# The first expert block and the last batch's attention steps of a two-layer kernel, in another order

## The chip, the cores and the metric

The kernel runs on one core of a Trainium2 chip. The core has a matrix engine (PE, whose weight loads are shown apart as PEld), three engines for elementwise work (DVE, ACT, POOL) and a queue for transfers (SP). POOL issues the scattered transfers too. Each engine runs its own instructions in their order and waits on semaphores for the others. The metric is the device time of one execution in microseconds (us), the median of several runs.

## The reference

The input is 8 batches of 512 tokens with 128 features. Two layers follow each other, each with a residual sum, `x = x + attention(xn) + ffn(xn)`. The first layer has a causal attention with 16 heads and a soft mixture of 8 experts. The second layer, in which the change lies, has a differential attention and a mixture of 8 experts that takes the two best experts for each token:

```python
# differential attention, per batch
diff = softmax(q1 @ k1.T * scale) - lam_full * softmax(q2 @ k2.T * scale)
out  = diff @ v
out / sqrt(mean(out * out) + EPS) * (1 - LAMBDA_INIT)
...
# experts: the rows sent to one expert stand together, at most 1280 of them
act     = gelu(einsum('ech,ehf->ecf', exp_in, moe_w1))     # 128 -> 512
exp_out = einsum('ecf,efh->ech', act, moe_w2)              # 512 -> 128
moe     = zeros.at[padded_ids].add(exp_out * padded_probs[:, None])
```

## The kernel before

Up to 874 us of the span the kernel does the first layer, the second layer's small attention and routing (which writes each token's row with its two weights and its number into the buffer `xs` in DRAM, line 910), and the differential attention of batches 0 to 6 (`diff`, line 1354). The differential attention of the eighth batch, number 7, is held back (`LATE`). It is a generator, `late`, and each `next` on it issues one step. There are 21: two products with the folded weights (`diff_qk`), one for the values (`diff_v`), eight scores (`diff_scores`: a product on PE of 512 columns, a maximum on DVE, an Exp on ACT), four with transposes (`diff_T`), one in which nothing is issued, four with the product with the values (`diff_out`, the last with four small operations on POOL, lines 1333 to 1336 and 129), and the end (`diff_end`, four rows on DVE, line 1342). `diff_both`, the difference of the two softmaxes on DVE, goes with a neighbouring step.

The rest of the kernel is the experts. Each of the 8 experts has 1280 slots, ten chunks of 128 rows, in three blocks of 4, 4 and 2 chunks; `BLOCKS` lists all 24. For each expert `rows_get` (line 1422) loads its rows into the tile `xe` on SP's queue, two experts ahead, and `rows_in` (line 1429) computes on DVE the weight and the token number of each row. For each block there are three steps.

- `expert_T` (line 1443): PE transposes the chunks, and DVE copies them with the layer norm's weight and bias into `xeT` (line 1447).
- `expert_up` (line 1451), called twice for a block: two products with the first weights on PE (line 1458; each is two matmul instructions in the trace) and a Gelu on ACT into `hT` (line 1461). Exp and Gelu need different tables in ACT; a load of the table is an instruction of its own in the trace.
- `expert_down` (line 1463), called for each half of the chunks: four products for each chunk into one tile of PSUM (line 1473; 16 instructions for two chunks). With the last half DVE scales each chunk into `es` (line 1481), and POOL adds each chunk's rows to the output by an indirect transfer (line 1486), 80 of them in all.

The stores of an expert may add to rows that the expert before has added to. So each store waits until all ten of the expert before have landed (lines 1493 and 1494). Batch 7's attention is added to the output by one direct transfer on POOL (`late_add`, lines 1503 to 1516) after the last block of expert 6. It waits for expert 6's stores and expert 7's stores wait for it.

What order the instructions of PE, DVE, ACT and POOL have is written by hand: `in_order` (line 244) ties each instruction to the one before it on its engine, as the program issues them. SP's queue isn't tied so. The loop at lines 1528 to 1542 is a pipeline. In block m it issues the two ups of block m+1, the transposes of block m+2, and the two halves of the down of block m, and, from block 6 on, two late steps in the first half and one in the second:

```python
for hp in range(2):
    expert_up(*BLOCKS[m + 1], hp)
    if hp == 1: expert_T(*BLOCKS[m + 2])      # rows_in first, for a new expert
    expert_down(e, c0, n, half[hp])
    late_steps(((2,1)[hp]) if m >= 6 else 0)
```

Ahead of the loop stand, in this order, the loads of experts 0 and 1, `rows_in(0)`, the transposes of blocks 0 and 1, and the two ups of block 0.

Of the kernel before, what the change touches and what calls it, by code (L numbers as in the profile page):

```python
# [18 lines left out]
P = 128  # L19
# [6 lines left out]
def kernel(ctx: ExitStack, tc: tile.TileContext, a: dict, out: bass.AP):  # L26
    nc = tc.nc
# [10 lines left out]
    CAP = 1280  # L38
    NCT = CAP // P
# [10 lines left out]
    def psum_s(name):  # L50
        return ps["s"].tile([P, 2, 512], F32, tag="s", name=name)

    def psum_o(name, pool="o"):
        return ps[pool].tile([P, 512], F32, tag="o", name=name)
# [9 lines left out]
    for b in range(NB):  # L64
# [9 lines left out]
        out=se, in_=a["L0_ffn_slot_embeds"].rearrange("e s d -> (e s) d").rearrange("(c p) d -> p c d", p=P)  # L74
# [10 lines left out]
    for n, key in enumerate(("L0_attn_qln_w", "L0_attn_qln_b", "L0_attn_kln_w", "L0_attn_kln_b")):  # L85
        nc.sync.dma_start(
            out=lnrow[n : n + 1], in_=a[key].unsqueeze(0).unsqueeze(0).to_broadcast([1, H, S])
# [10 lines left out]
    for e in range(NE):  # L98
        nc.sync.dma_start(
            out=b2c[(e % 2) * NS : (e % 2 + 1) * NS, e // 2, :],  # L100
            in_=a["L0_ffn_b2"][e : e + 1].to_broadcast([NS, D]),
# [10 lines left out]
    for n, v in enumerate((-0.5, -1.0)):  # L112
# [7 lines left out]
        out=cmask[:, 384:512], in_=cmask[:, 384:512], pattern=[[-1, P]],  # L120
# [17 lines left out]
    def transpose4(name, blocks, pool="t"):  # L138
        t = psum_t(name, pool)
        for k, blk in enumerate(blocks):  # L140
            nc.tensor.transpose(t[:, k * P : (k + 1) * P], blk, ident)  # L141
        return t

    xs = dram.tile([NE * CAP, W], F32, name="xs")
# [473 lines left out]
    sync = mybir.DependencyInfo(mybir.DependencyClass.Sync, mybir.DependencyReason.DATA)  # L618
    puts = []
# [622 lines left out]
    with ExitStack() as l1b:  # L1242
# [178 lines left out]

        def rows_get(e):
            xe = wk.tile([P, NCT, W], F32, tag="xe", name=f"xe_{e}", bufs=3)
            get = nc.sync.dma_start(out=xe, in_=xs[e * CAP : (e + 1) * CAP].rearrange("(c p) d -> p c d", p=P))
            for name in puts:
                tc.add_manual_dep(get.ins, name, sync, reason="any token may be in this expert's slots")
            ee["xe", e] = xe

        def rows_in(e):

            xe = ee["xe", e]
            first = small.tile([P, NCT], F32, tag="first", name=f"first_{e}", bufs=2)
            nc.vector.tensor_scalar(
                out=first, in0=xe[:, :, D + 3], scalar1=float((NE - e) * CAP), scalar2=None, op0=ALU.is_equal
            )
            wt_ = small.tile([P, NCT], F32, tag="wt", name=f"wt_{e}", bufs=2)
            nc.vector.tensor_tensor(out=wt_, in0=first, in1=xe[:, :, D + 1], op=ALU.mult)
            nc.vector.tensor_tensor(out=wt_, in0=wt_, in1=xe[:, :, D], op=ALU.add)
            to = small.tile([P, NCT], U32, tag="to", name=f"to_{e}", bufs=4)
            nc.vector.tensor_scalar(out=to, in0=xe[:, :, D + 2], scalar1=FAR, scalar2=None, op0=ALU.add)  # L1440
            ee["wt", e], ee["to", e] = wt_, to

        def expert_T(e, c0, n):
            w = n * P
            t = transpose4(f"xeT_p{e}_{c0}", [ee["xe", e][:, c0 + k, :D] for k in range(n)])
            ee["xeT", e, c0] = xeT = wk.tile([P, T], F32, tag="xeT", name=f"xeT_{e}_{c0}")
            nc.vector.tensor_scalar(  # L1447
                out=xeT[:, :w], in0=t[:, :w], scalar1=cols[:, 2:3], scalar2=cols[:, 3:4], op0=ALU.mult, op1=ALU.add
            )

        def expert_up(e, c0, n, hp):
            w, xeT = n * P, ee["xeT", e, c0]
            if hp == 0:
                ee["hT", e, c0] = wk.tile([P, NHC, T], F32, tag="hTm", name=f"hTm_{e}_{c0}")
            ph = psum_s(f"phm_{e}_{c0}_{hp}")
            for k in range(2):
                hc = 2 * hp + k
                nc.tensor.matmul(  # L1458
                    ph[:, k, :w], lhsT=w1_1[:, e, hc * P : (hc + 1) * P], rhs=xeT[:, :w], start=True, stop=True
                )  # L1460
            nc.scalar.activation(ee["hT", e, c0][:, 2 * hp : 2 * hp + 2, :w], ph[:, :, :w], AF.Gelu)  # L1461

        def expert_down(e, c0, n, ks):
            hT = ee["hT", e, c0]
            if c0 == 0 and ks[0] == 0:
                ee["es", e] = wk.tile([P, NCT, D], F32, tag="es", name=f"es_{e}", bufs=4)
                backs.append([])
            if ks[0] == 0:
                ee["pe"] = psum_o(f"pem_{e}_{c0}")
            pe, es = ee["pe"], ee["es", e]  # L1470
            for k in ks:
                for hc in range(NHC):
                    nc.tensor.matmul(  # L1473
                        pe[:, k * D : (k + 1) * D], lhsT=hT[:, hc, k * P : (k + 1) * P], rhs=w2_1[:, e, hc, :],
                        start=(hc == 0), stop=(hc == NHC - 1),
                    )
            if ks[-1] < n - 1:
                return
            for k in range(n):
                c = c0 + k  # L1480
                nc.vector.tensor_scalar(
                    out=es[:, c], in0=pe[:, k * D : (k + 1) * D], scalar1=ee["wt", e][:, c : c + 1], scalar2=None,
                    op0=ALU.mult,
                )

                back = nc.gpsimd.indirect_dma_start(  # L1486
                    out=out_rows, out_offset=bass.IndirectOffsetOnAxis(ap=ee["to", e][:, c : c + 1], axis=0),
                    in_=es[:, c], in_offset=None, bounds_check=NB * T - 1, oob_is_err=False,
                    compute_op=ALU.add,
                )  # L1490
                tc.declare_no_dep(back.ins, group=f"backs{e}", reason="an expert's rows differ")
                tc.add_to_no_dep_group(f"backs{e}", back.ins)
                for name in backs[e] if e else bases:
                    tc.add_manual_dep(back.ins, name, sync, reason="a row is read and written by each addition")
                backs[e + 1].append(back.ins.name)
# [3 lines left out]
        def late_steps(n):  # L1499
            for _ in range(n):  # L1500
                next(late, None)

        def late_add(e):

            for _ in late:
                pass
            new = []
            for b in LATE:
                add = nc.gpsimd.dma_start(
                    out=out[b].rearrange("(i p) d -> p i d", p=P),  # L1510
                    in_=dd["po", b].rearrange("p (i d) -> p i d", i=NI), accum_op=ALU.add,
                )
                for name in backs[e + 1]:
                    tc.add_manual_dep(add.ins, name, sync, reason="a row is read and written by each addition")
                new.append(add.ins.name)
            backs[e + 1] = new

        BLOCKS = [(e, c0, min(4, NCT - c0)) for e in range(NE) for c0 in range(0, NCT, 4)]
        AFTER = 6
        rows_get(0)  # L1520
        rows_get(1)
        late_steps(0)
        rows_in(0)
        expert_T(*BLOCKS[0])
        expert_T(*BLOCKS[1])
        expert_up(*BLOCKS[0], 0)
        expert_up(*BLOCKS[0], 1)
        for m, (e, c0, n) in enumerate(BLOCKS):
            if c0 == 0 and e + 2 < NE:
                rows_get(e + 2)  # L1530
            half = range(n // 2), range(n // 2, n)
            for hp in range(2):
                if m + 1 < len(BLOCKS):
                    expert_up(*BLOCKS[m + 1], hp)
                if hp == 1 and m + 2 < len(BLOCKS):
                    if BLOCKS[m + 2][1] == 0:
                        rows_in(BLOCKS[m + 2][0])
                    expert_T(*BLOCKS[m + 2])
                expert_down(e, c0, n, half[hp])
                late_steps(((2,1)[hp]) if m >= 6 else 0)  # L1540
            if e == AFTER and c0 + n == NCT:
                late_add(e)
        in_order(tail)
# [37 lines left out]
```

## Time and profile before

| what | value |
|---|---|
| median of 3 runs | 1081.13 us (1080.82 to 1083.46) |
| the profiled execution | 1080.87 us |
| its span, first to last instruction | 1079.2 us |
| PE busy over the span | 964.9 us (89%) |
| DVE, ACT, POOL busy over the span | 677.6, 561.3, 569.0 us |
| PE and POOL busy from 897 to 1053 us | 153.9 and 111.9 of 156 us |
| PE and POOL busy from 1053 us to the end | 0.0 and 15.5 of 26.2 us |
| stores of the experts (line 1486) | 80, mean 1555 ns, from 897.7 to 1073.5 us |
| table loads in the experts' part | 7 for Gelu, 6 for Exp, 1283 ns each |

The span is what the profile covers; the execution's time is 1.67 us longer than its span. Times inside the span are counted from its start. A row of the timeline has the start and duration of an instruction or of a few merged ones, its engine, its line, the operation, what it writes and reads, and, in brackets, how long its engine sat idle before it and which instruction released it. An engine's idle time counts only where it delays what ends last. For that the chain of waits is followed back from the last instruction.

### The profile page before, as it was taken

The numbers are of one execution on the slowest core, as the hardware profiler recorded it, in microseconds if no ns is written. First come the engines' busy times: TensorE is split into PE (matmuls) and PEld (weight loads), VectorE is DVE, ScalarE is ACT, GpSimd is POOL, SyncE is SP. The second block draws the span as 40 slices with busy tenths as digits, with TensorE's granted clock in tenths as the row PEclk, the third lists the DMA queues.
The fourth block names the chain that finished last, engine by engine and source line by source line (L and its number), as shares of the span: only waits on it lengthen the run. The fifth ranks groups of instructions, "written<-read, shape, count | busy, mean of one in ns | idle before, by whom it ended". The sixth has DMA issues, their size and how long they took to land.

```text
span 1079.2 us, 18766 instructions
## 1 busy us (share of the span) xinstructions
PE 964.9 (89%) x6702; PEld 594.3 (55%) x6702; DVE 677.6 (63%) x2130; ACT 561.3 (52%) x1261; POOL 569.0 (53%) x794
## 2 busy tenths in 40 slices
PE   7889899989999999999899999878678879999990
PEld 3457556857545455545444445345445657777780
DVE  6634643377777788888878788359887642243230
ACT  3466347363366566767565655526346552393220
POOL 3201000200242537785878978876877635667775
PEclk9899999999699999999999999859889999999995
DMA  8630000000000000000000000050000143332213
GB/s 253 153 92 2 1 1 1 2 1 2 1 1 2 1 2 2 19 4 2 9 14 2 22 1 22 2 173 1 10 20 16 30 110 58 50 50 36 26 10 34
DMA packets 49838, 33.23 MB, mean 31 GB/s; under 512 B 12248, under 2 KB 44803, under 8 KB 49744
## 3 DMA queue, kind: packets, MB, share of 16 engines
q1 hardware_dynamic: 34832, 24.80, 8.6%
q0 software_dynamic: 14096, 6.97, 4.9%
q8 instruction: 53, 0.87, 0.3%
q14 instruction: 41, 0.34, 0.1%
q10 hardware_dynamic: 816, 0.26, 0.1%
HBM read 17.56 MB, written 17.33 MB: 32 GB/s over the span
## 4 chain that ended last, share of the span: by engine, by line
PE 62%; POOL 13%; DVE 13%; issue 5%; ACT 3%; DMA 2%; POOLq 0%; SPq 0%; DVEq 0%; ACTq 0%
PE se L1082 11%; PE phm L1458 6%; PE pem L1473 6%; PE po L1107 5%; PE sm L1049 4%; PE lg_d L316 3%; PE pe L491 3%; PE psl L360 3%; DVE junk L1059 3%; PE s L1287 3%; PE pf L393 2%; POOL xs L910 2%; PE pq L969 2%; PE lg_c L316 2%; PE ph L465 2%
## 5 line engine op out<-in xcount | busy, mean ns | idle before, releaser
L1059 DVE CUSTOM_DVE_ANT_0 junk<-sm,cmask 128x128 f32<-128x128 f32 (+3 forms) x512 | 249.7, 488 | 68.9 <-PE sm L1049 30.5
L1087 ACT ACTIVATE pt<-se 128x384 f32<-128x384 f32 (+1 forms) x384 | 185.7, 527 | 158.7 <-PE sm L1049 110.0
L1049 PE MATMUL sm<-kj,qT 32*128 32x256 f32 (+3 forms) x1024 | 231.5, 483 | 5.4 <-ACT kj L643 2.7
L1082 PE MATMUL se<-q,kj 32*128 32x128 f32 (+3 forms) x1024 | 210.2, 477 | 4.0 <-DVE mcol L1059 3.5
L1486 POOL DMA_INDIRECT out_dram<-es,to x80 | 124.4, 1555 | 61.9 <-issue 28.4
L1082 PEld LDWEIGHTS se<-q,kj 32*128 32x128 f32 x1024 | 99.8, 189 | 86.9 <-DVE mcol L1059 25.2
L1092 POOL TENSOR_SCALAR_AFFINE_SELECT pt<-pt 128x512 f32<-128x512 f32 (+1 forms) x96 | 80.0, 833 | 115.2 <-ACT pt L1087 115.0
L1049 PEld LDWEIGHTS sm<-kj,qT 32*128 32x128 f32 x1024 | 111.4, 190 | 24.4 <-DVE mcol L1059 10.3
L1107 PE MATMUL po<-pt,vpad 128*18 128x512 f32 (+3 forms) x1024 | 92.0, 455 | 12.0 <-POOL pt L1092 12.0
L1461 ACT ACTIVATE hTm<-phm 128x1024 f32<-128x1024 f32 (+1 forms) x48 | 42.4, 882 | 79.0 <-PE phm L1458 78.8
L1458 PE MATMUL phm<-xeT,w 128*128 128x512 f32 (+1 forms) x192 | 78.7, 534 | 4.1 <-DVE xeT L1447 3.6
L1473 PEld LDWEIGHTS pem<-w,hTm 128*128 128x128 f32 x640 | 77.0, 192 | 7.6 <-issue 7.2
L1291 ACT ACTIVATE ex<-s,nm 128x512 f32<-128x512 f32 x64 | 43.9, 687 | 69.2 <-DVE nm L1290 68.7
L1473 PE MATMUL pem<-w,hTm 128*128 128x128 f32 x640 | 78.9, 275 | 0.0
L910 POOL DMA_INDIRECT xs<-l_z,sput x64 | 67.3, 1051 | 17.9 <-issue 15.4
L1287 PE MATMUL s<-xn,qk 128*128 128x512 f32 x128 | 69.4, 662 | 7.1 <-ACT qk L1265 3.9
L522 POOL TENSOR_TENSOR x_all<-x_all,bo_bc 128x512 f32<-128x512 f32 x8 | 10.2, 1276 | 121.4 <-DVE xn L280 121.4
L1447 DVE TENSOR_SCALAR xeT<-xeT_p,cols 128x512 f32<-128x512 f32 (+1 forms) x24 | 17.2, 721 | 73.9 <-PE xeT_p L141 73.9
L1107 PEld LDWEIGHTS po<-pt,vpad 128*18 128x18 f32 x1024 | 20.7, 97 | 62.8 <-POOL pt L1092 23.7
L1290 DVE TENSOR_REDUCE nm<-s 128x1 f32<-128x512 f32 x64 | 43.0, 683 | 17.0 <-PE s L1287 16.7
L1458 PEld LDWEIGHTS phm<-xeT,w 128*128 128x128 f32 x192 | 34.0, 194 | 27.0 <-issue 21.6
L736 POOL TENSOR_TENSOR l_prod<-l_qkv 128x512 f32<-128x512 f32 x36 | 46.3, 1298 | 3.2 <-DVE l_at L630 1.9
(270 smaller groups left out, 1872.4 us busy)
## 6 DMA issues: line engine op xcount, KB each, us to landing
xs<-cmask SPq DMA_DIRECT2D x1, 5280.0 KB, 24.1
xe<-xs SPq DMA_DIRECT2D x8, 660.0 KB, 4.4
x_all<-in_L_attn_x_dram SPq DMA_DIRECT2D x8, 256.0 KB, 4.6
w<-in_L_ffn_w_dram SPq DMA_DIRECT2D x1, 2048.0 KB, 8.9
w<-in_L_ffn_moe_w_dram SPq DMA_DIRECT2D x1, 2048.0 KB, 9.8
out_dram<-x_all SPq DMA_DIRECT2D x8, 256.0 KB, 2.2
out_dram<-es,to POOLq DMA_INDIRECT x80, 3.2
xs<-l_z,sput POOLq DMA_INDIRECT x64, 2.3
```

Of the source, the lines that this page charges most:

```text
L316: nc.tensor.matmul(lg, lhsT=lhs(k), rhs=rhs, start=True, stop=True)
L910: put = nc.gpsimd.indirect_dma_start(out=xs, out_offset=bass.IndirectOffsetOnAxis(ap=sput[:, k, m : m + 1], axis=0), in_=z2[:, i], in_offs ...
L1049: nc.tensor.matmul(sc[:, o : o + w], lhsT=st["qT", b][rr, i * P : (i + 1) * P], rhs=st["k", b, j][rr, :w], start=True, stop=True,)
L1059: nc.vector.tensor_tensor_reduce(out=junk[:, :w], in0=sc[:, o : o + w], in1=cmask[:, 512 - w : 512], scale=-1.0, scalar=BIG, op0=ALU.add, ...
L1082: nc.tensor.matmul(sc[:, o : o + w], lhsT=st["k", b, j][rr, c * P : (c + 1) * P], rhs=st["q2", b, (g % G) // 2][rr, c * P : T], start=True ...
L1087: nc.scalar.activation(st["pt", g, k][:, r, :o], sc[:, :o], AF.Exp)
L1092: nc.gpsimd.affine_select(out=pt[:, :, :n, :P], in_=pt[:, :, :n, :P], pattern=[[0, 4], [0, n], [1, P]], compare_op=ALU.is_ge, fill=0.0, ba ...
L1107: nc.tensor.matmul(po[32 * r : 32 * r + 2 * PW, c * P : T], lhsT=vpads[b % 3][:, c, at_ : at_ + 2 * PW], rhs=pt[:, r, o : o + w], start=(c ...
L1287: nc.tensor.matmul(sc, lhsT=dd["qk", b, k][:, i * P : (i + 1) * P], rhs=xnT[:, b], start=True, stop=True)
L1458: nc.tensor.matmul(ph[:, k, :w], lhsT=w1_1[:, e, hc * P : (hc + 1) * P], rhs=xeT[:, :w], start=True, stop=True)
L1473: nc.tensor.matmul(pe[:, k * D : (k + 1) * D], lhsT=hT[:, hc, k * P : (k + 1) * P], rhs=w2_1[:, e, hc, :], start=(hc == 0), stop=(hc == NH ...
L1486: back = nc.gpsimd.indirect_dma_start(out=out_rows, out_offset=bass.IndirectOffsetOnAxis(ap=ee["to", e][:, c : c + 1], axis=0), in_=es[:, ...
```

## The change

It has three parts. The load of expert 0's rows is split into two transfers, of four and of six chunks. In front of the loop block 0's transposes go ahead of `rows_in(0)`, and block 1's transposes go behind block 0's ups; block 0's whole down, with its es and its four stores, then comes ahead of the ups of block 1 and the transposes of block 2. The late steps are issued one per block, in its first half, from block 3 on. By block 20 that is 18 steps; the remaining three (the last two products with the values, with the four small operations on POOL, and the end) are issued in `late_add`, which runs the generator to its end.

```diff
         def rows_get(e):
             xe = wk.tile([P, NCT, W], F32, tag="xe", name=f"xe_{e}", bufs=3)
-            get = nc.sync.dma_start(out=xe, in_=xs[e * CAP : (e + 1) * CAP].rearrange("(c p) d -> p c d", p=P))
-            for name in puts:
-                tc.add_manual_dep(get.ins, name, sync, reason="any token may be in this expert's slots")
+            rows = xs[e * CAP : (e + 1) * CAP].rearrange("(c p) d -> p c d", p=P)
+
+            for c0, c1 in ((0, 4), (4, NCT)) if e == 0 else ((0, NCT),):
+                get = nc.sync.dma_start(out=xe[:, c0:c1], in_=rows[:, c0:c1])
+                for name in puts:
+                    tc.add_manual_dep(get.ins, name, sync, reason="any token may be in this expert's slots")
...
         late_steps(0)
+        expert_T(*BLOCKS[0])
         rows_in(0)
-        expert_T(*BLOCKS[0])
-        expert_T(*BLOCKS[1])
         expert_up(*BLOCKS[0], 0)
         expert_up(*BLOCKS[0], 1)
+        expert_T(*BLOCKS[1])
         for m, (e, c0, n) in enumerate(BLOCKS):
...
             half = range(n // 2), range(n // 2, n)
+            if m == 0:
+
+                expert_down(e, c0, n, range(n))
             for hp in range(2):
...
-                expert_down(e, c0, n, half[hp])
-                late_steps(((2,1)[hp]) if m >= 6 else 0)
+                if m > 0:
+                    expert_down(e, c0, n, half[hp])
+                late_steps(((1,0)[hp]) if m >= 3 else 0)
```

## The prediction

> **What bounds the kernel now.** The change lies behind 874 us, so I read the end of the chain of waits first. From 884 us on it runs through PE at line 1473 and line 1458 block after block, and only from 1035 us through POOL's stores (line 1486). So I put the timelines of POOL, DVE and ACT beside each other. Columns: start, duration, engine, line, operation, and in brackets the idle time before it with its releaser.
>
> ```profile
> 897.68 1.68 POOL L1486 DMA_INDIRECT out_dram<-es,to  x1 [16.05 <-DVE es L1481]
> ...
> 914.53 1.55 POOL L1486 DMA_INDIRECT out_dram<-es,to  x1 [0.31 <-issue]
> 919.67 1.55 POOL L1486 DMA_INDIRECT out_dram<-es,to  x1 [3.58 <-issue]
> ...
> 957.63 1.61 POOL L1486 DMA_INDIRECT out_dram<-es,to  x1 [0.30 <-issue]
> 965.15 1.55 POOL L1486 DMA_INDIRECT out_dram<-es,to  x1 [5.92 <-DVE es L1481]
> ...
> 982.10 1.55 POOL L1486 DMA_INDIRECT out_dram<-es,to  x1 [0.30 <-issue]
> ...
> 989.53 1.64 POOL L1486 DMA_INDIRECT out_dram<-es,to  x1 [2.15 <-DVE es L1481]
> ...
> 1047.85 1.54 POOL L1486 DMA_INDIRECT out_dram<-es,to  x1 [0.30 <-issue]
> 1051.35 1.39 POOL L1509 DMA_DIRECT2D out_dram<-po  x1 [1.96 <-DMA out_dram<-es,to]
> 1056.76 1.64 POOL L1486 DMA_INDIRECT out_dram<-es,to  x1 [4.03 <-DMA out_dram<-po]
> ```
>
> The 80 stores on POOL are the spine from 897.68 to the end. Ten stores of an expert take 16.6 to 17.0 us from first to last start. Then the next expert waits until they have landed: from last start to next start 5.14 (into expert 1), 4.32 (2), 4.70 (5) and 3.68 us (6), mean 4.46. Two steps are longer, 7.52 us into expert 3 and 7.43 us into expert 4, and there DVE's es is the releaser: PE was late. For expert 3 the row on DVE is:
>
> ```profile
> 964.52 1.13 DVE L1481 TENSOR_SCALAR es<-pem,wt 128x128 f32<-128x128 f32 x4 [1.24 <-PE pem L1473]
> ```
>
> The first es of experts 0 to 7 start at 897.04, 916.01, 936.69, 964.52, 988.89, 1007.86, 1026.82 and 1045.79. Without late steps PE needs 18.96 us per expert (1007.86 to 1026.82), less than POOL's 21.1. With the late steps of batch 7 crowded into blocks 6 to 12 it took 27.83 and 24.37. So PE bounds experts 3 and 4, the landing of the stores all others.
>
> **The first block.** Before it, this row order on DVE decides:
>
> ```profile
> 881.67 1.13 DVE L1347 SCALAR_TENSOR_TENSOR x_all<-po,ri,x_all 128x128 f32<-128x128 f32 x4 [5.30 <-POOL ri L129]
> 882.71 0.17 DVE L1433 TENSOR_SCALAR first<-xe 128x10 f32<-128x10 f32 x1
> ...
> 883.29 1.52 DVE L1447 TENSOR_SCALAR xeT<-xeT_p,cols 128x512 f32<-128x512 f32 x2
> ```
>
> *Split load.* I cost it at nothing: PE transposes xe at 879.55, so it has landed by then, and DVE is shut until 882.7 by batch 6's last rows. One more SP issue (0.36 us) stands ahead of expert 1's load, which isn't read before some 901.8. If that cover went, the earlier landing would be worth at most what 396 of 660 KB take at some 300 GB/s, 1.3 us.
>
> *Transposes ahead of rows_in.* Four DVE operations (882.71 to 883.29) leave the front of xeT: 0.58 us earlier. PE starts line 1458 at 883.57 instead of 884.15; eight matmuls took 5.24 us (half of it at a granted clock of 0.5), so they end at 888.81, and the second gelu ends at 890.03 (890.61 before).
>
> *Block 0's down in one go.* Block 1's transposes (0.44) now stand here, then PE waits for that gelu, idle some 0.95 us, which block 1's up covered before. The 32 down matmuls take 3.73 us (the row at 1049.10): 890.2 to 893.93. es starts then, the first store 0.64 later as before: 894.6, 3.1 us earlier. But block 1 pays: two ups 3.44, T 0.22, then PE waits for xeT (1.1 us from the transposes' start) where a down covered it before, 0.86 idle; up 0.87, two half downs 3.58 with up and T (1.30) between, 0.17 to the last one's end. es of block 1 starts at 904.25, before 902.78: **1.47 later**. POOL, through its first four stores at 901.9, waits for it: fifth store 904.88 (905.26 before), tenth 914.15 (914.53). So of 3.1 us some 0.4 are left.
>
> **The late steps.** The generator has 21 steps. Before: three a block from block 6, done at 12. After: one a block from 3 to 20, and the last three (two out steps, the end) in late_add. PE prices from starts in the trace: a score or qk 0.86, v 0.89, four transposes 0.43, out 0.89. I set each expert's first es, by PE, against POOL (last start + 4.46), es + 0.64 giving the store:
>
> - expert 1: PE 916.01 + 1.47 + 0.86 (qk) = 918.34, store 918.98; POOL 918.61. Start 918.98.
> - expert 2: + 18.96 + 0.86 + 0.89 + 0.86 = 939.91, store 940.55; POOL 918.98 + 16.72 + 4.46 = 940.16. Start 940.55 (940.71 before).
> - expert 3: + 18.96 + three scores 2.58 + 0.9 stall (below) = 962.35, store 962.99; POOL 961.93. Start 962.99 (965.15).
> - expert 4: + 18.96 + 2.15 = 983.46, store 984.10; POOL 962.99 + 16.95 + 4.46 = 984.40. Start 984.40 (989.53).
> - expert 5: POOL 1005.58, PE 1004.78. Expert 6: POOL 1026.65, PE 1025.49. Start 1026.65 (1031.24).
>
> **The table loads.** Dealt singly, eight scores switch ACT between Exp and Gelu 16 times, before 12 times. What decides is whether a load waits for the exp's data:
>
> ```profile
> 941.86 1.28 ACT L1291 ACT_TABLE_LOAD   x1 [2.76 <-DVE nm L1290]
> ...
> 946.53 1.28 ACT L1291 ACT_TABLE_LOAD   x1
> 948.23 0.69 ACT L1291 ACTIVATE ex<-s,nm 128x512 f32<-128x512 f32 x1 [0.42 <-DVE nm L1290]
> ```
>
> Only the first did (it has a separate semaphore instruction, the last of that line at 941.8); the one at 946.53 ran ahead. With T0 the start of a score on PE: exp at T0 + 1.83, gelu 2.15 after it, 0.6 or 1.02 long: hT is ready at T0 + 4.63 to 5.05. PE, with up, T, half down and up between, asks for it at T0 + 5.46, 5.67 or 5.88, by the block's place in its expert: no stall. The first one, 1.28 later, stalls PE 0.9. If all loads waited, the stalls would be 0.9, 0.2 and 0.45 by place, 3.75 in all for blocks 6 to 11, 13 and 14. Bounds 0 and 3.75; I take 0.9, by the row at 946.53.
>
> **The addition of batch 7.** Its four ri operations now stand on POOL behind expert 6's tenth store, 1043.26. From the rows at 982.10 and after: store 1.55, ri ready 3.53 after the store's start, DVE's four rows 1.05, release 0.3: the addition starts 4.88 after that store, where landing alone needed 3.50. **Cost 1.38.** The outs on PE end near 1040, some 4 us before POOL asks. Addition at 1048.14 instead of 1051.35; what follows (5.41, ten stores, the end) is unchanged.
>
> **Sum.** 3.2 us off the profiled span of 1079.2: 1076.0. That execution took 1080.87 us, 1.67 around the span and 0.26 below the median of 1081.13. On the median: **1077.9 us**. Everything hangs on two near ties, PE against POOL, at 0.1 to 1.2 us.
>
> **Rivals.**
>
> *All Exp loads wait for data* (above): 2.85 more on PE, expert 6 at 1028.34, 2.9 earlier than before, less 1.38: **1079.6**. For it: 27 of 48 gelus and the first exp have a separate wait. Against it: the five later loads all began before their nm had ended. 0.2.
>
> *PE's clock doesn't drop in the first block.* It did after an idle time of 3.56 us (880.59 to 884.15), and came back within 888 to 889; the granted clock is the third number from the end of this stretch:
>
> ```profile
> 885.00:886.00 1.00, 1.00 (x2) 0.34 (x1) 0.00 (x0) 0.00 (x0) 0.00 (x0) 0.53 0.04 8
> ```
>
> Now PE is idle 0.07 us less (0.44 later transposes, 0.58 earlier start: 880.08 to 883.57, 3.49). A shorter idle time, 874.7 to 876.5, left the clock at 1.00. Without the drop the first four matmuls end at 885.4 (four at 0.43 and 0.15), the load (1.28) and two gelus (2.17) behind them at about 889.0, 1.0 earlier, and PE, which bounds experts 1 to 3, carries that through: **1076.9**. 0.2. The Trainium skill (TensorE: Matmul & The Clock Gate, "What's actually happening") says that a free-running window of about 3.4 us that is idle halves the clock, and a busy one restores it; the trace's drop, 885.0 to 888.4, is as long, and by that rule 3.49 us of idle time may or may not hold such a window.
>
> *A switch of tables costs more than its load.* This is the way to the slower side. Its place is each score step, between exp and gelu. With x us more per switch, the first of a pair is hidden up to 1.1, the second takes the spare 0.41, 1.04 and 0.83 by place. The nearest row for x is the load itself, 1.28. Both together then delay hT by 1.45: stalls of 1.04, 0.41 and 0.62, 5.2 in all, and 2.4 more at the unhidden first load; PE is then 6.7 beyond my sum at expert 6, which starts at 1032.2: **1083.4**, and over 1084.4 from x = 1.34 on. It is slower than before once PE is 4.4 beyond my sum there. Against it: the load at 946.53 starts 0.01 after the gelu before it, and the gelu behind the load of 949.09 at 950.38, 0.01 after the load's end. 0.08. The Trainium skill (ScalarE: Activation LUTs, "What ACT_TABLE_LOAD costs") gives 1283 ns for the load, as here, and some 1.38 us of draining besides, which by the working above would make some 1085; by its advice to batch by set, dealing scores out singly is the wrong direction. No row here shows the draining.
>
> **How the numbers follow.** Forecast 0.52, waiting loads 0.2, no drop 0.2, dearer switches 0.08. The forecast's own spread is about 1.2 us: a landing wait of 3.7 or 5.1 instead of 4.46 moves the boundaries behind expert 3 by up to 0.7 each, and PE's lead, 0.3 to 1.2 us, caps the gain. A change of 0.3% (3.24 us, to 1077.89) is about what a measurement of this kernel can tell from none, and the forecast lies on that line: half of it counts as faster, half as same. Faster 0.26 + 0.2 = 0.46; same 0.26 + 0.2 and a quarter of the dearer switches, 0.48; slower 0.06. The range runs from 1075.0 (no drop, no stall at the first load, and landings so short that PE alone bounds expert 6: 1.0, 0.9 and 1.2 less, rounded) to 1081.2 (all loads waiting, 1079.6, and landings of 5.1 behind expert 3); outside lie the dearer switches and some 5 in 100 on either side.
>
> **What would show it.** First store near 894.6 from the span's start (allowing for a shift of all that lies before 874), but a gap of about 3 us between the fourth and fifth; PE idle before the first line 1473 and before block 2's line 1458. Starts of experts 3, 4 and 6 earlier by about 2, 5 and 4.6. 16 table loads, Exp's ahead of their data but for one, and no PE wait on ACT beyond 1 us. Lines 1335 and 129 behind expert 6's tenth store, and about 4.9 us from that store to the addition. I am wrong if PE's 18.96 us per expert without late steps isn't kept, if waits on ACT appear at each score, or if the landing waits grow because expert loads (after each expert's first transposes) now meet the last stores of the expert before.

## The result and the profile after

The changed kernel takes **1077.85 us** (median of 12 runs, 1071.45 to 1081.73), the kernel before 1081.93 (12 runs beside them, 1079.95 to 1085.97). The ratio is 0.9957 with a 95% interval of 0.9937 to 0.9976: 4.7 us less, between 2.6 and 6.8 (the two medians lie 4.1 apart). The profiled execution took 1075.83 us with a span of 1074.1, before 1080.87 with 1079.2.

Both kernels run the same code up to batch 6's last rows on DVE (line 1347), but the execution that was profiled reached them at 881.67 us before and 882.70 after, and the kernels below at 879.15 to 884.55. So the part that the change touches is compared from there: **B6** is the start of those rows in each profile. From B6 to the end of the span it was 197.53 us, now 191.40: 6.1 less.

POOL's timeline of the changed kernel (start, duration, engine, line, operation, idle time before it and its releaser). The experts' lines stand 3 lower in the file, so a store is line 1489 and es line 1484.

```profile
894.01 1.67 POOL L1489 DMA_INDIRECT out_dram<-es,to  x1 [11.35 <-DVE es L1484]
...
904.36 1.55 POOL L1489 DMA_INDIRECT out_dram<-es,to  x1 [3.09 <-DVE es L1484]
...
913.65 1.55 POOL L1489 DMA_INDIRECT out_dram<-es,to  x1 [0.31 <-issue]
918.44 1.55 POOL L1489 DMA_INDIRECT out_dram<-es,to  x1 [3.25 <-DVE es L1484]
...
940.02 1.55 POOL L1489 DMA_INDIRECT out_dram<-es,to  x1 [3.31 <-DVE es L1484]
...
962.06 1.55 POOL L1489 DMA_INDIRECT out_dram<-es,to  x1 [3.75 <-DVE es L1484]
...
983.18 1.55 POOL L1489 DMA_INDIRECT out_dram<-es,to  x1 [2.85 <-DVE es L1484]
...
1003.86 1.55 POOL L1489 DMA_INDIRECT out_dram<-es,to  x1 [2.42 <-DVE es L1484]
...
1024.59 1.55 POOL L1489 DMA_INDIRECT out_dram<-es,to  x1 [2.46 <-DVE es L1484]
...
1041.30 1.55 POOL L1489 DMA_INDIRECT out_dram<-es,to  x1 [0.30 <-issue]
...
1043.79 1.04 POOL L129 TENSOR_TENSOR ri<-ri,powers 128x4 f32<-128x4 f32 x1
1046.04 1.41 POOL L1512 DMA_DIRECT2D out_dram<-po  x1 [1.21 <-DVE po L1342]
1051.69 1.66 POOL L1489 DMA_INDIRECT out_dram<-es,to  x1 [4.25 <-DMA out_dram<-po]
```

The first store comes early and a gap of 3.09 us follows behind the fourth, as the prediction had it. But at the first store of each of experts 1 to 6, not only of 1 to 3, the releaser is now DVE's es, which waits for PE: up to the addition of batch 7, POOL has nothing left to wait for but PE. The windows from 908 to 1042 us say the same (columns: length, then busy time and number of instructions of PE, PEld, DVE, ACT and POOL, granted clock, DMA share, GB/s). Before:

```profile
908.00:1042.00 134.00, 132.05 (x785) 99.83 (x784) 46.50 (x133) 59.58 (x81) 95.59 (x65) 1.00 0.29 38
```

After:

```profile
908.00:1042.00 134.00, 133.15 (x794) 101.15 (x793) 45.91 (x129) 65.98 (x85) 98.53 (x64) 1.00 0.29 38
```

PE's idle time in it has gone from 1.95 to 0.85 us. PE was nearly full before, too: what changed is that no crowd of late steps makes it late for one expert and early for the next. The starts, counted from B6 ("drop" is the kernel no_split below, which differs from the change by the split of one load that is worth nothing, and in whose profile the clock drops as the prediction assumed):

| from B6, us | before | predicted | change | drop |
|---|---|---|---|---|
| first and fifth store | 16.01, 23.59 | 12.9, 23.2 | 11.31, 21.66 | 12.48, 22.83 |
| expert 1 | 38.00 | 37.3 | 35.74 | 36.90 |
| expert 2 | 59.04 | 58.9 | 57.32 | 58.48 |
| expert 3 | 83.48 | 81.3 | 79.36 | 80.52 |
| expert 4 | 107.86 | 102.7 | 100.48 | 101.64 |
| expert 5 | 129.28 | 123.9 | 121.16 | 122.32 |
| expert 6 | 149.57 | 145.0 | 141.89 | 143.06 |
| addition of batch 7 | 169.68 | 166.5 | 163.34 | 164.52 |
| first store of expert 7 | 175.09 | 171.9 | 168.99 | 169.86 |
| end | 197.53 | 194.3 | 191.40 | 192.31 |

### The profile page after: what moved, and what is told of

Read it like the earlier page. It is cut to its first block, busy times and chain, and to the rows that moved or that the text cites. A ratio compares the mean times of both kernels' runs of the same rounds, so it can differ in the third digit from the quotient of the medians.

```text
span 1074.1 us, 18776 instructions
## 1 busy us (share of the span) xinstructions
PE 961.3 (89%) x6702; PEld 593.6 (55%) x6702; DVE 677.1 (63%) x2130; ACT 566.4 (53%) x1265; POOL 567.8 (53%) x794
## 4 chain that ended last, share of the span: by engine, by line
PE 62%; DVE 14%; POOL 13%; issue 5%; ACT 4%; DMA 2%; POOLq 0%; DVEq 0%; ACTq 0%
PE se L1082 11%; PE phm L1461 6%; PE pem L1476 6%; PE po L1107 5%; PE sm L1049 4%; PE lg_d L316 3%; DVE junk L1059 3%; PE pe L491 3%; PE psl L360 3%; PE pf L393 2%; PE lg_c L316 2%; PE pq L969 2%; POOL xs L910 2%; PE ph L465 2%; PE s L1287 2%
## 5 line engine op out<-in xcount | busy, mean ns | idle before, releaser
L1107 PE MATMUL po<-pt,vpad 128*18 128x512 f32 (+3 forms) x1024 | 89.2, 443 | 13.7 <-POOL pt L1092 13.7
```

The source lines that it names most:

```text
L1107: nc.tensor.matmul(po[32 * r : 32 * r + 2 * PW, c * P : T], lhsT=vpads[b % 3][:, c, at_ : at_ + 2 * PW], rhs=pt[:, r, o : o + w], start=(c ...
```

## The experiments

**Theory**: the late steps' new places take PE's two late arrivals away, the first block's early start is mostly given back, and what bounds the time then is PE. **Rival**: the landing of each expert's last store bounds it (the prediction's 4.46 us), and PE only at experts 1 to 3. Starts and steps come from one profiled execution of each kernel, the ratios (each with its 95% interval) from up to 12 runs beside runs of the kernel before.

### Each part alone

late_only is the kernel before with the new places of the late steps; first_only is the change with the old ones:

```diff
-                late_steps(((2,1)[hp]) if m >= 6 else 0)
+                late_steps(((1,0)[hp]) if m >= 3 else 0)
```

> The kernel before with only the late steps dealt out as in the change. Theory A (the gain is all from the late steps, PE is what each expert's start waits for, and the new first block costs PE some 1.5 us): about 6 us faster than before, 1 to 1.5 us faster than the whole change; experts 1 to 6 start when their es is there, expert 6 some 7.5 us earlier than before. Theory B (the prediction as written, landings of 4.46 us bound experts 4 to 6): about 4 us faster than before. Theory C (the gain comes from the early first stores): within 1 us of before, because the stores start at 897.7 as before.

> The kernel before with only the split load and the new first block; late steps three a block from block 6. Theory A: first store 3 us earlier, but es of block 1 some 1.5 us later, experts 3 and 4 wait for PE that much longer, and the end is 1 to 1.5 us later than before (less, if PE's clock happens not to drop in the first block). Theory B: the same, PE bounds experts 3 and 4 in it too. Theory C: 3 to 4 us faster than before.

late_only: 0.995 (0.9927 to 0.9973), B6 to the end 193.65. first_only: 1.0008 (0.9992 to 1.0023), 198.25. So the late steps make the gain, and the new first block alone makes none: its first store came at 12.48 from B6, expert 2 at 56.73, 2.3 earlier than before, and at expert 3 all was lost, because the crowded late steps made PE late as before (step from last to first store 7.53 us).

By the ratios the two parts add up (0.995 times 1.0008 is 0.9958, and the change has 0.9957). In the profiles they don't: -3.9 and +0.7 apart, and -5.2 together with the clock drop. In its profile late_only has lost time at its boundaries. Its last store of expert 0 and first of expert 1:

```profile
917.95 1.55 POOL L1486 DMA_INDIRECT out_dram<-es,to  x1 [0.30 <-issue]
923.81 1.55 POOL L1486 DMA_INDIRECT out_dram<-es,to  x1 [4.31 <-issue]
```

and SP's queue, the load of expert 4's rows (the fifth of the eight loads):

```profile
918.48 0.36 SPq L1424 DMA_DIRECT2D xe<-xs  x1
```

It waits for the buffer of expert 1's rows: PE's last transposes of that expert end at 918.45 (the prediction had put the loads behind an expert's first transposes). The load begins 0.53 us behind the last store, and the next expert starts 5.86 us after that store. At the next two boundaries loads stand 0.46 and 0.45 us ahead of the last store, and the steps are 5.28 and 5.16; at 1.2 us ahead 4.17; with none 3.57 and 3.70. In the change the loads begin 2.0 to 2.9 us behind it, and es is the releaser. That loads could meet the last stores was named in the prediction as a sign of being wrong; it came in late_only, not in the change.

### The loads kept away from the last stores

late_gate is late_only, after_gate the change, with the loads from expert 2's on held back: an expert's load is issued one block later and waits until the first store of the expert two before it has landed:

```diff
-        def rows_get(e):
+        def rows_get(e, behind=()):
...
-                for name in puts:
+                for name in puts + list(behind):
...
-            if c0 == 0 and e + 2 < NE:
-                rows_get(e + 2)
+            if c0 == 4 and e + 2 < NE:
+                rows_get(e + 2, backs[e + 1][:1])
```

> The kernel before with the late steps dealt out as in the change, and each load of an expert's rows from the third on held back until the first store of the expert two ahead of it has landed, so that no load stands beside an expert's last store. Theory D (a load issued within half a us of an expert's last store lengthens that store's landing by 1.5 to 2.3 us; with the dealt steps alone this bounds experts 1 to 3, and the new first block avoids it by shifting stores against loads): the steps into experts 1 to 3 fall from 5.9, 5.3 and 5.2 to where PE sets them, at most 4.6 us; from batch 6's last rows to the end 191.4 instead of 193.7 us, the changed kernel's value without counting the clock. Rival: the landings are as long without loads; then 193.7 stays.

> The changed kernel with the loads held back in the same way. Theory D: nothing beyond 0.3 us, since its loads already come 2 to 3 us after the last store and PE sets every start. Rival (loads lengthen the waits here too): about 1 us faster. Should the clock drop in the first block as it does in most profiles, some 0.9 us more than in the changed kernel's own profile.

late_gate: 0.9954 (0.994 to 0.9969), end at 191.65 from B6. after_gate: 0.9956 (0.9938 to 0.9975), 192.20. late_gate's boundary into expert 1:

```profile
916.64 1.55 POOL L1486 DMA_INDIRECT out_dram<-es,to  x1 [0.30 <-issue]
920.21 1.55 POOL L1486 DMA_INDIRECT out_dram<-es,to  x1 [2.01 <-DVE first L1433]
```

The step is 3.57 us there instead of 5.86, and es bounds all later ones. So without the new first block, but with the loads out of the way, the profile ends as early as with it: what the new first block did in the change's profile was to move the stores away from the loads, and PE's bound is the same for both. after_gate gains nothing over the change, since PE bounds it already. The ratios of the four kernels (0.995 to 0.9957) are too close to each other to show this (their intervals are 3 to 5 us wide), and late_only's isn't above the others: it rests on one profile of each, and that the new first block is worth anything in the median isn't shown.

### The split load

no_split is the change with one transfer for expert 0:

```diff
-            for c0, c1 in ((0, 4), (4, NCT)) if e == 0 else ((0, NCT),):
+            for c0, c1 in ((0, NCT),):
```

> The changed kernel with expert 0's rows loaded in one transfer. Theories A and B: the same as the whole change within what can be told (0.3 us), with the first transposes of xe starting as soon as PE has ended batch 6's last product, and DVE free only after batch 6's last rows. If the split load counts, this is up to 1.3 us slower, and the first transposes of xe wait for a DMA.

0.996 (0.9944 to 0.9976), 1077.41 us: the split does nothing, as costed.

### The clock in the first block

In no_split's profile the eight matmul instructions of the two ups of block 0 take 5.40 us on PE:

```profile
884.98 5.40 PE L1461 MATMUL phm<-xeT,w 128*128 128x512 f32 x8 [3.42 <-DVE xeT L1450]
```

and in the change's they take 3.70, behind the same idle time of 3.42 us:

```profile
884.61 3.70 PE L1461 MATMUL phm<-xeT,w 128*128 128x512 f32 x8 [3.42 <-DVE xeT L1450]
...
889.03 0.71 PE L1476 MATMUL pem<-w,hTm 128*128 128x128 f32 x4 [0.29 <-ACT hTm L1464]
889.95 3.39 PE L1476 MATMUL pem<-w,hTm 128*128 128x128 f32 x28 [0.20 <-ACT hTm L1464]
...
897.72 1.10 PE L1461 MATMUL phm<-xeT,w 128*128 128x256 f32 x4 [0.73 <-DVE first L1436]
```

The granted clock from 887 to 888 us is 0.50 in no_split and 1.00 in the change. The idle times before the first down (0.29 and 0.20) and before block 2's ups (0.73) are the two that the prediction had named (at 0.95 and 0.86). Of the seven kernels here with that idle time of 3.42 us the clock dropped in six; the change's own profile is the exception. It dropped in all three with 3.56 or 3.57 (before, late_only, late_gate). after_warm puts three products that nobody reads into the idle time, ahead of the ups:

```diff
         expert_T(*BLOCKS[0])
+        hot = psum_t("hot")
+        for _ in range(3):
+            nc.tensor.matmul(hot, lhsT=ident, rhs=cmask, start=True, stop=True)
         rows_in(0)
```

> The changed kernel with three products of 512 columns on PE, whose result isn't used, between block 0's transposes and its ups, so that PE isn't idle for 3.4 us there. If the idle time is what halves the clock: granted clock 1.0 through the first block, the eight products of block 0's ups in 3.7 instead of 5.4 us, first store 11.3 us after batch 6's last rows instead of 12.5, and the end 0.9 us earlier than in a run with the drop, as in the changed kernel's own profile. If the drop has another cause, 5.4 and 12.5 us.

0.9945 (0.9928 to 0.9963), first store at 11.30 and end at 191.02 from B6:

```profile
881.39 2.74 PE L1529 MATMUL hot<-cmask,ident 128*128 128x512 f32 x6
884.98 3.70 PE L1461 MATMUL phm<-xeT,w 128*128 128x512 f32 x8 [0.84 <-DVE xeT L1450]
```

The idle time is 0.84 us and the ups run at full clock; so they do in the two other kernels with these three products (below). Against no_split's 192.31 that is 1.3 us in the profile; the medians don't separate it from the change.

### The late steps taken out, and the addition at the very end

no_late is the change without the late steps: it leaves batch 7's attention out and adds zeros in its place by the same transfer. add_last has batch 7's addition behind expert 7 instead of 6 (`AFTER = 7`).

> The changed kernel without any late step: batch 7's differential attention is left out, zeros are added in its place by the same transfer. PE then needs 18.96 us per expert, so nothing but the landing of the stores holds POOL, and the wait from an expert's last store to the next one's first can be read. Theory A: 3.5 to 3.9 us in the middle, expert 6 near 1021 counted as before, 10 us faster than before. Theory B: 4.46 us in the mean, expert 6 near 1024.6, 6.5 us faster than before.

> The changed kernel with batch 7's addition behind expert 7 instead of expert 6. From expert 6's last store to expert 7's first the step falls from 10.4 to some 4 us (PE sets it); the four small operations now stand among expert 7's stores, about 1.8 us; the addition starts 3.5 us after the last store and lands about 5 us later. In sum 1 to 1.5 us faster than the changed kernel. Rival: the small operations hold POOL until PE's last products are done, and the gain is given back.

no_late: 0.9916 (0.9893 to 0.9939), 1072.38 us, end at 187.48 from B6. So the 21 steps cost the changed kernel 4.8 us (192.31 less 187.48, both with the clock drop). That may be too little, for POOL isn't free in no_late either: into expert 2 a load begins 0.1 us ahead of the last store and the step is 5.42 us, with es not the releaser.

add_last: 0.9969 (0.995 to 0.9987), end at 194.01, which is 1.7 later than with the addition behind expert 6 (192.31). This missed: I had expected 1 to 1.5 us less. Expert 7's first store came at 164.25 instead of 169.86, but then:

```profile
1054.59 1.04 POOL L129 TENSOR_TENSOR ri<-ri,powers 128x4 f32<-128x4 f32 x1
1055.83 1.65 POOL L1489 DMA_INDIRECT out_dram<-es,to  x1 [0.20 <-issue]
...
1065.18 1.54 POOL L1489 DMA_INDIRECT out_dram<-es,to  x1 [0.31 <-issue]
1069.19 1.38 POOL L1512 DMA_DIRECT2D out_dram<-po  x1 [2.48 <-DMA out_dram<-es,to]
```

The small operations on POOL stand between expert 7's stores (18.64 us from first to last, otherwise 16.75). The addition waits 4.0 us for the landing of the last store, and the span ends 7.11 us after it began, where a last store needs 5.7. The small operations cost 1.9 us (1.8 expected); what the expectation had too low is the rest: 5 us for the addition's landing (7.11 to the end), 3.5 us ahead of it (4.0) and a step of 4 us to expert 7's first store (4.5).

### PE as the bound: the late steps dealt to where PE has time

If PE bounds every expert, late steps should go where nobody waits for PE: few into experts 1 to 5, and most into the blocks of expert 6 and the next, since expert 7's stores wait for the addition anyway. sparse deals them so (ten by expert 6's first es, eight in blocks 18 to 20, and the last three in `late_add`), with the loads held back as in after_gate and the three products of after_warm:

```diff
+        DEAL = {(4, 0): 1, (5, 0): 1, (6, 0): 1, (7, 0): 1, (9, 0): 1, (10, 0): 1, (12, 0): 1, (14, 0): 1, (16, 0): 1,
+                (17, 0): 1, (18, 1): 1, (19, 0): 1, (19, 1): 2, (20, 0): 2, (20, 1): 2}
...
-                late_steps(((1,0)[hp]) if m >= 3 else 0)
+                late_steps(DEAL.get((m, hp), 0))
```

sparse_old is the same with the old order of the first block; deal_only is the change with this dealing alone.

> The changed kernel with the loads held back, PE kept busy ahead of block 0's ups, and the late steps dealt out by what PE can spare: three by expert 2's first es, five by expert 3's, seven, eight and ten by those of experts 4, 5 and 6, ten more in blocks 18 to 20. If PE is what sets the starts of experts 2 to 6 in the changed kernel and landings without a load beside them take 3.5 to 3.7 us: expert 6 starts 137.5 to 139.5 us after batch 6's last rows (141.9 in the changed kernel's own profile), batch 7's addition at 161 to 162.5 (163.3), and the end at 188.5 to 190 (191.4). Rival (landings, not PE, set the starts in the changed kernel): expert 6 stays near 142.

> The same with the first block, the load of expert 0's rows and the order of the ups as in the kernel before. The old order leaves PE some 1.1 us further ahead at block 1, the new one starts the stores of expert 0 earlier. If both are worth what the runs so far show, expert 1 starts 0.9 us later than in the run with the new block, and the difference at the end is under 1 us either way. If the early first stores are what pays, the end is more than 1 us later.

> The changed kernel with the late steps dealt out as in the run that spares PE (three by expert 2, five, seven, eight and ten by experts 3 to 6, ten more in blocks 18 to 20), but with the loads where the changed kernel has them and without the added products ahead of block 0. If the dealing alone is what pays: the end 188.5 to 190 us after batch 6's last rows, with up to 1 us of that for the clock's drop in the first block, and steps into experts 3 and 4 near 4.2 and 3.7 us as there. If the loads, which then come 1 to 2 us after an expert's last store, lengthen its landing: steps of 4.6 us and more into experts 3 and 4, and an end past 190.

sparse: **0.9903 (0.9877 to 0.9928), 1072.15 us**, the fastest kernel of this study, end at 187.99 from B6 (188.5 to 190 expected). Experts 3 to 6 and the addition start at 77.36, 97.82, 118.09, 138.73 and 160.25 (137.5 to 139.5 expected for expert 6, 161 to 162.5 for the addition). Its first stores of experts 3, 4, 5 and 6 and the addition:

```profile
961.67 1.55 POOL L1489 DMA_INDIRECT out_dram<-es,to  x1 [2.61 <-DVE es L1484]
...
982.13 1.55 POOL L1489 DMA_INDIRECT out_dram<-es,to  x1 [2.19 <-DVE es L1484]
...
1002.40 1.55 POOL L1489 DMA_INDIRECT out_dram<-es,to  x1 [2.01 <-DVE es L1484]
...
1023.04 1.55 POOL L1489 DMA_INDIRECT out_dram<-es,to  x1 [2.17 <-DVE es L1484]
...
1044.56 1.41 POOL L1512 DMA_DIRECT2D out_dram<-po  x1 [1.21 <-DVE po L1342]
```

es is still the releaser, but the idle times of 2.19, 2.01 and 2.17 at experts 4 to 6 (2.85, 2.42 and 2.46 in the change) are about the shortest that any boundary of these kernels shows (1.95 to 2.2): the landing is now as late as PE. The end is 0.5 later than no_late's, whose clock dropped; 1 us for that drop added, sparse is some 1.5 us behind a kernel without late steps. Its loads are held back and no_late's aren't, so this isn't the price of the steps alone.

sparse_old: 0.9944 (0.9925 to 0.9962), end at 191.73. This missed: I had expected less than 1 us between the two, and it is 3.7 in the profile. Expert 1 starts 1.9 later (36.80 against 34.88), and the steps into experts 1 to 4 take 4.88, 5.12, 4.90 and 4.64 us although no load is near. The first of them:

```profile
914.09 1.55 POOL L1486 DMA_INDIRECT out_dram<-es,to  x1 [0.30 <-issue]
918.97 1.55 POOL L1486 DMA_INDIRECT out_dram<-es,to  x1 [3.33 <-issue]
```

and the DMA queues from 912 to 919.5 us (packets, MB, share):

```profile
q0 software_dynamic: 432, 0.00, 2.9%
q8 instruction: 1, 0.02, 0.8%
```

One packet of a queue that brings instructions (q8) comes 2.0 us behind the last store; at the other three boundaries 1.8 to 1.9 us behind it. Into experts 5 and 6, where the next of that queue comes 4.7 and 4.0 us behind, the steps are 3.56 and 3.68. Before has a step of 4.70 and first_only of 4.74 into expert 5 with such a packet 1.5 and 1.7 us behind the store and no load. Where one comes 2.8 us or more behind it, or before it, and no load is near, the step stays short (late_only into expert 5: 3.6 us behind, 3.57; no_late into expert 4: 2.8 us behind, 3.49). A packet of the other instruction queue (q14) 0.7 us behind the store, in sparse_old into expert 6, didn't lengthen the step either.

deal_only: 0.9932 (0.9919 to 0.9945), 1075.30 us, end at 191.75 in its profile, where the clock dropped (the profiled execution, 1077.13 us, is the slowest of its six). Dealing alone takes little off the profile of no_split (192.31): the step into expert 3 is 4.3 us with es as the releaser, so the longer landing expected there doesn't show; into expert 4 its load begins 1.19 us behind the last store and the step is 4.80, and from the addition to expert 7's first store it takes 6.12 us (5.25 in sparse). So what sparse has over the change isn't the dealing alone: the loads held back and the clock kept up are part of it, though each of them alone gave the change little (after_gate, after_warm). deal_only's median lies between the change's and sparse's, its interval overlaps both.

## Why the prediction held, point by point

- **Sum.** 3.2 us less was forecast, 4.7 (2.6 to 6.8) measured. That the medians almost meet (1077.9 and 1077.85) is partly chance: the kernel before was 0.8 slower beside the change than in the three runs that the sum stood on, and with the ratio those would give 1076.5. In the profile it is 5.2 with the clock drop that the sum assumed and 6.1 without. The range's upper end, 1081.2, is some 0.6 above what its two terms give by the prediction's own steps (all loads waiting and landings of 5.1 put expert 6 near 1029.3, which is 1080.6); nothing hangs on it.
- **The mis-sized term** is "the landing of the stores", taken as "mean 4.46" of four steps. That mean was a mixture. A step with nothing beside it takes 3.5 to 3.7 us; the longer ones had a load near the last store (into experts 1 and 2, 0.3 and 1.5 us ahead of it) or an instruction packet (into expert 5). So "PE bounds experts 3 and 4, the landing of the stores all others" doesn't hold after the change: PE bounds experts 4 to 6 as well, at 101.64, 122.32 and 143.06 with the drop. PE's own part was forecast nearly to the hundredth: from expert 4 to 5 and from 5 to 6 it took 20.68 and 20.73 us, and by the prediction's prices 20.68 and 20.71. At expert 6 the forecast (1026.65) is 1.9 late; by PE alone (1025.49) it would have been 0.8 late, so 1.2 are this term; the 0.8 are block 1's es (below) and the first table load's stall, 0.4 each.
- **The first block.** "3.1 us earlier" and "1.47 later" were 3.5 earlier and 1.08 later (no_split's first store and block 1's es). Mechanism and sign hold: most of the gain is given back at the fifth store, and what is left is 0.8 instead of 0.4 us. Most of the difference is the wait for the second gelu, put at 0.95 us: in no_split PE is idle for 0.23 us there, because the first four down instructions run ahead of that wait (0.61 us, at 890.65).
- **The late steps.** Experts 3 and 4 were to start 2.2 and 5.1 earlier and started 3.0 and 6.2 earlier with the drop. PE kept its 18.96 us per expert plus the prices of the late steps, and no new wait took the place of the one removed.
- **The table loads.** Only the first Exp load waits for data; the next runs ahead of it. ACT's timeline of the change:

```profile
936.44 1.28 ACT L1291 ACT_TABLE_LOAD   x1 [2.33 <-DVE nm L1290]
937.73 0.69 ACT L1291 ACTIVATE ex<-s,nm 128x512 f32<-128x512 f32 x1
...
941.35 1.28 ACT L1291 ACT_TABLE_LOAD   x1
944.13 0.69 ACT L1291 ACTIVATE ex<-s,nm 128x512 f32<-128x512 f32 x1 [1.49 <-DVE nm L1290]
```

  The load at 941.35 ends 1.5 us before its exp has its data. The first one's stall on PE was 0.5 instead of 0.9 us (22.04 between the first es of experts 2 and 3, 22.44 forecast), and the longest wait of PE on ACT there is 0.24. So the rivals "All Exp loads wait for data" and "A switch of tables costs more than its load" fall. The draining that the Trainium skill (ScalarE: Activation LUTs, "What ACT_TABLE_LOAD costs") adds to each load doesn't show: from the load at 936.44 to the next instruction there is 0.01 us, the load at 941.35 starts 0.02 us behind the end of the gelu before it, and 16 switches beside the experts cost PE some 0.5 us in all.
- **The addition.** 4.88 us from expert 6's last store was forecast, 4.74 measured; ri was ready 3.53 after that store's start, as worked out.
- **PE's clock.** The rival "PE's clock doesn't drop in the first block" was put at 0.2. It happened in the change's profiled execution and in none of the six others with the same idle time; its price was 1.2 us at the first store and 0.9 at the end, 1.0 forecast. The traces show what goes with it. In every profile here all switches of the granted clock lie whole multiples of 3.41 us apart. On the grid of such stretches that this gives, the one that ended with the drop held 1.05 us of PE's work in no_split; in the change the idle time fell on two stretches, with 1.59 and 1.48 us of work (columns as in the windows above, PE's busy time behind the length):

```profile
882.61:886.03 3.42, 1.05 (x3) 0.57 (x4) 2.36 (x9) 0.00 (x0) 0.44 (x1) 1.00 0.55 161
...
879.26:882.67 3.41, 1.59 (x12) 1.36 (x12) 0.00 (x0) 0.65 (x4) 1.24 (x2) 1.00 1.16 318
882.67:886.08 3.41, 1.48 (x4) 0.76 (x5) 2.36 (x9) 0.00 (x0) 0.00 (x0) 1.00 0.43 127
```

  The first row is no_split's. In the nine profiles with the drop PE was idle for 2.3 to 3.0 us of that stretch, in the change for 1.9 at most. So by the traces the exception was luck, in where the idle time fell on this grid; no run moved the grid by itself. The Trainium skill (TensorE: Matmul & The Clock Gate, "What's actually happening") has a free-running window of about 3.4 us that halves the clock when it is idle: the traces agree with its length and that it doesn't start with the idle time, but the window needn't be idle throughout.

What stays open: at late_only's first four boundaries an instruction packet comes as well, 2.9 to 4.1 us behind the last store. A load alone does lengthen the step (no_late into expert 2, where the packet comes only at 4.7 us: 5.42), but whether the packets add to it in late_only wasn't separated. That the packets at 1.5 to 2.0 us are the cause of sparse_old's longer steps is argued from where they stand; no run moved them alone.

## What to carry to other kernels

When a wait is taken as a mean over several places, look first at what else moves at each place: four "equal" waits of 3.7 to 5.1 us look like one wait of 3.5 to 3.7 with different neighbours. Work that fills a bounded engine should be dealt out by who is waiting for that engine: here the steps belonged where nothing waits for PE. The same 21 steps ended the kernel 4.8 us behind the one without them in one dealing, and about 1.5 in another that also held the loads back and kept the clock up; the dealing alone took 0.6 us off the profile. An earlier start of one block can be worth nothing by itself and still shift transfers into or out of each other's way, so measure the parts of such a change alone and together.

## What the runs showed of the hardware

- Where a load of 660 KB begins within some 0.5 us of a store of 128 rows, the step that waits for the store's landing takes 5.1 to 5.9 us instead of 3.5 to 3.7. Holding the loads back brought it from 5.86 to 3.57 us (late_gate). Where one packet of the instruction queue q8 comes 1.5 to 2.0 us behind the store and no load is near, it took 4.6 to 5.1 us (seen, not tried out).
- The same idle time of PE, 3.42 us, dropped the granted clock to 0.5 in six profiles of seven, which is 5.40 instead of 3.70 us for the two ups; three products in the gap kept it at 1.00 in three of three. The switches of the clock lie on a grid of 3.41 us, and the drop came where PE was idle for 2.3 us or more of one stretch of it (nine profiles), and not at 1.9 (one).
- A direct addition at the end of the kernel needs 7.11 us from its start to the end of the span, the last scattered store 5.7.
